# Sharing the copies of a pair of pieces five to three, and pairing pieces across two units in the third block

## The chip, the cores and the metric

The kernel runs on one core of a Trainium2 chip. The metric is the device time of one execution in microseconds (us); several runs are timed and their median is given. One further execution is recorded by the hardware profiler, and all the profile's rows come from it.

## What is computed

An encoder-decoder layer in fp32. The encoder works on 77 context rows per batch; the decoder on 2 batches of 2048 rows of width 512, 16 heads of 32. The change lies in the decoder's causal self-attention:

```python
yn = _ln(y, dec_n1_s, dec_n1_b)
y = y + _mha(yn, yn, dec_sa_in_w, ..., sb)      # sb: relative bias and causal mask
# in _mha:
scores = jnp.einsum('bhqd,bhkd->bhqk', q, k) / jnp.sqrt(hd) + bias[None]
attn = jax.nn.softmax(scores, axis=-1)
out = jnp.einsum('bhqk,bhkd->bhqd', attn, v)
```

After it come cross-attention to the encoder's output and a feed-forward layer, which the change does not touch.

## The kernel before

**Units and pieces.** A batch's 2048 rows are four blocks m = 0 to 3 of 512 rows. The self-attention of a block is cut into 16 *units* (b, m, g, t): g is one of four groups of four heads, t one of four tiles of 128 query rows. Units are numbered through: block 1 of the first batch is units 16 to 31, block 2 ("the third block") 32 to 47, block 3 48 to 63; the second batch's are 64 later. A unit looks at i + 1 = 4m + t + 1 tiles of 128 keys, cut into *pieces* of up to four tiles by `pieces`: in block 2, t = 0 has pieces of 4, 3 and 2 tiles, t = 1 4, 4, 2, t = 2 4, 4, 3 and t = 3 4, 4, 4. Block 3 has four pieces in each unit, block 1 two. `stream` is the list of all pieces in order.

**What is done to a piece.** Four steps, each a function:

- `scores` (L353): one matmul for each of the four heads, each into a PSUM bank of its own. VectorE takes them out (L362, and L369 with the bias for the last two tiles) with a running maximum. After a unit's last piece its four exponentials on ScalarE (L379, one per head over the whole width of the unit) can run; for m > 0 they are put in a list, `late_exps`, and called a few at a time by `exps`.
- `turn` (L389 to L412): transposes the probabilities. A *load* is four transposes (one key tile, four heads) into one bank, and a copy of that bank to `pts`, by ScalarE (L409) or by VectorE (L407). The first half of a turn's loads (rounded up) is ScalarE's. Behind the fourth load's copy one exponential of the next unit is called (L410, L411), and another at the end.
- `values` (L420): the products with `vv`, into the eighth bank, which is kept for them.
- `slot` (called once per unit): other work laid out by hand over the units: projections (L206, L217, L230), the output product (L242), norms, divisions, and in the early units the encoder's stages. Each has its loads by DMA, issued up to three jobs ahead.

**Banks.** `bank()` hands out seven banks in rotation to scores, loads and slots' jobs alike, in the order in which the program calls it. Each engine runs its instructions in the order of the program (`manual_schedule`), and a matmul waits for the engine that last read its bank.

**The main loop** (in the listing below, from L1249) takes up to two pieces of the same unit as a *pair*: it makes sure that the unit is fully scored and its exponentials are called, turns the pair, runs the next unit's slot if the pair ends the unit, scores one more piece ahead if `may_score` allows, calls one exponential (two in block 1), does the pair's values, and after a pair of two scores further pieces as far as `may_score` allows. `may_score` lets a unit be scored where the unit two before it has been turned, as both lie in the same half of `pp`. A unit of block 2 is thus a pair and a left-over piece; a unit of block 3 is two pairs, of which the first is followed by a score directly and the second by a slot.

Of the kernel before, what the change touches and what calls it, by code (L numbers as in the profile page):

```python
# [54 lines left out]
def tile_encoder_decoder(ctx: ExitStack, tc: tile.TileContext, ins, out):  # L55
# [93 lines left out]
    with (  # L149
# [20 lines left out]
        def bank():  # L170

            i = count["bank"] % count["banks"]
            count["bank"] += 1
            return psum[:, i, :]

        def in_turn(what, tile):
            i = count[what] % tile.shape[1]
            count[what] += 1
            return tile[:, i, :]
# [116 lines left out]
        def pieces(i):  # L296


            n = i + 1
            if n % 4 == 1 and n > 1:  # L300
                sizes = [4] * ((n - 5) // 4) + [3, 2]
            else:
                sizes = [4] * (n // 4) + ([n % 4] if n % 4 else [])
            out, k0 = [], 0
            for s in sizes:
                out.append((k0, s))
                k0 += s
            return out

        units = [(b, m, g, t) for b in range(B) for m in range(NMB) for g in range(NC) for t in range(TB)]  # L310
        stream = [(n, k0, kn) for n, u in enumerate(units) for k0, kn in pieces(u[1] * TB + u[3])]
# [17 lines left out]
        late_exps = []  # L329

        def exps(k):

            for _ in range(min(k, len(late_exps))):
                late_exps.pop(0)[1]()
# [54 lines left out]
        def turn(pieces):  # L389

            first = units[pieces[0][0]][1] == 0
            loads = []
            for n, k0, kn in pieces:
                ks = range(k0, k0 + kn)
                if first:
                    loads += [[(n, k, r) for k in ks] for r in range(HC)]
                else:
                    loads += [[(n, k, r) for r in range(HC)] for k in ks]
            for o, load in enumerate(loads):
                pt = bank()  # L400
                pts = in_turn("pts", pts_all).rearrange("p (x q) -> p x q", q=P)
                for x, (n, k, r) in enumerate(load):
                    nc.tensor.transpose(pt[:, ts(x, P)], state[n]["p"][r][:, ts(k, P)], ident)  # L403
                    got[n, k, r] = pts[:, x, :]
                w = len(load) * P
                if o % 2 if first else o >= (len(loads) + 1) // 2:
                    nc.vector.tensor_copy(pts[:, : len(load), :], pt[:, :w])  # L407
                else:
                    nc.scalar.copy(pts[:, : len(load), :], pt[:, :w])  # L409
                if o == min(3, len(loads) - 1):  # L410
                    exps(1)  # L411
            exps(1)  # L412

        def values(n, k0, kn):
            b, m, g, t = units[n]
            i = m * TB + t
            for k in range(k0, k0 + kn):
                ot = psum[:, 7, :].rearrange("p (t q) -> p t q", q=P)
                for r in range(HC):
                    nc.tensor.matmul(  # L420
                        ot[rows4(r), t, :], vv[:, k, ts(g * HC + r, HD)], got.pop((n, k, r)),
                        start=(k == 0), stop=(k == i),
                    )
                if t == TB - 1 and k == i:
                    o = ots[b, m, g] = in_turn("oT", oT_all)
                    (nc.vector.tensor_copy if m else nc.scalar.copy)(o, psum[:, 7, :])
# [459 lines left out]
        ahead = {n: [] for n in range(-1, len(units) + NU)}  # L886

        for x, (b, m) in enumerate(blocks):
            u = x * NU
            first = m == 0  # L890
# [12 lines left out]
            for t in range(TB):  # L903
                end = x == len(blocks) - 1
# [26 lines left out]
        def load_next():  # L931

            while len(loaded) < min(len(queue), ran[0] + (5 if ran[0] < 4 else 3)):
                ahead = [queue[i][2] for i in range(ran[0], len(loaded) + 1)]
                if sum(ahead) > 2:
                    break
                loaded.append(queue[len(loaded)][0]())
# [27 lines left out]
        def slot(n):  # L965
            for f in light[n]:
                f()
            for _, run, _ in jobs[n]:
                load_next()
                run(loaded[ran[0]])  # L970
                ran[0] += 1
# [35 lines left out]
        def w_1_load(i):  # L1007

            nc.sync.dma_start(w_1[:, :, ts(i, D)], wchunk("dec_ff1_wT", i * D))
# [217 lines left out]
        end = len(units)  # L1227
        size = [m * TB + t + 1 for b, m, g, t in units]
        turned_to, scored_to, at = {n: 0 for n in range(end)}, {}, [0]

        def may_score():

            if at[0] == len(stream):
                return False
            n, k0, kn = stream[at[0]]
            same = n >= 2 and units[n][:2] == units[n - 2][:2]
            return n < 2 or turned_to[n - 2] >= (min(k0 + kn, size[n - 2]) if same else size[n - 2])

        def score_next():
            n, k0, kn = stream[at[0]]  # L1240
            scores(n, k0, kn)
            scored_to[n] = k0 + kn
            at[0] += 1
# [4 lines left out]
        i = 0  # L1248
        while i < len(stream):  # L1249
            n = stream[i][0]  # L1250
            pair = [p for p in stream[i : i + 2] if p[0] == n]
            while scored_to.get(n) != size[n]:
                score_next()
            while any(u == n for u, _ in late_exps):
                exps(1)
            ends = pair[-1][1] + pair[-1][2] == size[n]
            if ends:
                for f in ahead[n + 1]:
                    f()
            turn(pair)  # L1260
            if n == end - 2:
                for _, k0, _ in pair:
                    w_1_load(k0 // 4)
            turned_to[n] = pair[-1][1] + pair[-1][2]
            if ends and n + 1 < end:
                slot(n + 1)
            if may_score():
                score_next()
            exps(2 if units[n][1] == 1 else 1)
            for p in pair:  # L1270
                values(*p)
            while may_score() and (len(pair) > 1 or units[n][1] == 0):
                score_next()
            i += len(pair)

# [68 lines left out]
```

## Time and profile before

| what | us |
|---|---|
| median of 3 runs | 2958.81 (2956.04 to 2960.45) |
| the profiled execution: its own time | 2958.76 |
| the profiled execution: span from first to last instruction | 2957.0 |
| block 1, first batch (196.4 to 413.6) | 217.2 |
| block 2, first batch (413.6 to 646.9) | 233.3 |
| block 3, first batch (646.9 to 934.9) | 288.0 |
| blocks 1, 2, 3 of the second batch | 200.5, 233.4, 275.9 |

The cuts are the first transposes of each block; the first batch's blocks hold the encoder's stages and the second's parts of the cross-attention in their slots. The last block is taken to 1785.5, some 5 us after its last transpose; behind it comes the feed-forward phase, to the end. In the profile PE is TensorE's matmul and PEld its weight load, DVE is VectorE, ACT is ScalarE, POOL is GpSimd. A timeline row gives the start, the length, the engine, the line, the operation, output <- input with shapes, how many were merged, and in brackets the engine's idle time ahead of it with what ended it. A row of several merged instructions gives their common length. The granted TensorE clock was 0.987 over the span.

### The profile page before, as it was taken

Reading aid. Unit: us, or ns where it says so; the run is one execution under the profiler, and the core shown is the slowest. Engines: PE = TensorE matmul, PEld = TensorE weight load, DVE = VectorE, ACT = ScalarE, POOL = GpSimd, SP = SyncE. Lnnn points to the kernel's source line nnn. Section 1 sums busy time; section 2 is a strip of 40 time slices with the busy share of each in tenths; the row PEclk is TensorE's granted clock in tenths of the full one; section 3 lists DMA queues with packets and bytes.
Section 4 is the critical chain, followed back from the end, with each engine's and each line's share of the span. In section 5 each row is a group of like instructions: output and inputs, shape, how many; then the busy total and the mean of one; then the engine's idle time right before and its main releaser. Section 6 shows DMA issues by size and latency. Waiting matters only on the chain.

```text
span 2957.0 us, 60689 instructions
## 1 busy us (share of the span) xinstructions
PE 2875.8 (97%) x24440; PEld 2018.7 (68%) x24440; DVE 2202.4 (74%) x6171; ACT 1220.9 (41%) x2211; POOL 737.2 (25%) x601
## 2 busy tenths in 40 slices
PE   8899999999999999999999997999999999999999
PEld 5456666666666556666666675777777777777788
DVE  4767688888987788888878884767676777776765
ACT  3344456546665455555556671213131313131311
POOL 0100000000000101000000004464646464646464
PEclk9799999999999999999999999999999999999999
DMA  6313301201112502201101124000001000000000
GB/s 175 87 52 118 102 16 51 66 16 44 34 41 69 129 19 79 70 26 62 41 16 37 45 75 156 1 29 1 29 1 37 10 29 1 29 1 29 1 15 15
DMA packets 117643, 137.10 MB, mean 46 GB/s; under 512 B 18240, under 2 KB 73072, under 8 KB 117234
## 3 DMA queue, kind: packets, MB, share of 16 engines
q1 hardware_dynamic: 117362, 133.22, 15.5%
q8 instruction: 192, 3.15, 0.5%
q14 instruction: 89, 0.73, 0.1%
HBM read 111.33 MB, written 21.86 MB: 45 GB/s over the span
## 4 chain that ended last, share of the span: by engine, by line
PE 79%; DVE 13%; DMA 3%; issue 2%; POOL 2%; ACT 2%; SPq 0%; POOLq 0%; DVEq 0%; ACTq 0%
PE psum L1152 13%; PE psum L403 12%; PE psum L353 9%; PE psum L1121 8%; PE psum L420 7%; DVE pp L362 5%; PE psum L230 4%; PE psum L806 4%; PE psum L746 4%; PE psum L206 4%; PE psum L242 4%; PE psum L217 3%; DVE pp L369 3%; PE psum L786 2%; PE psum L797 1%
## 5 line engine op out<-in xcount | busy, mean ns | idle before, releaser
L379 ACT ACTIVATE pp<-pp,nm 128x128 f32<-128x128 f32 (+15 forms) x512 | 614.6, 1210 | 200.8 <-DVE nm L376 198.2
L362 DVE TENSOR_SCALAR_CACHE_REDUCE pp<-psum 128x512 f32<-128x512 f32 (+3 forms) x1024 | 558.3, 590 | 47.2 <-PE psum L353 45.3
L403 PE MATMUL psum<-ident,pp 128*128 128x128 f32 x4352 | 549.6, 279 | 18.3 <-DVE mx L369 11.8
L403 PEld LDWEIGHTS psum<-ident,pp 128*128 128x128 f32 x4352 | 475.1, 142 | 132.3 <-DVE pp L362 57.1
L409 ACT COPY pts<-psum 128x512 f32<-128x512 f32 (+3 forms) x592 | 299.1, 577 | 509.6 <-PE psum L403 400.6
L1104 POOL TENSOR_TENSOR vv<-pp 128x512 f32<-128x512 f32 x320 | 415.6, 1316 | 137.4 <-PE psum L1121 117.7
L407 DVE COPY pts<-psum 128x512 f32<-128x512 f32 (+2 forms) x544 | 329.9, 660 | 42.1 <-PE psum L403 39.3
L353 PE MATMUL psum<-kT,q 32*128 32x512 f32 (+3 forms) x2560 | 352.1, 579 | 4.6 <-ACT kT L222 1.6
L420 PEld LDWEIGHTS psum<-pts,vv 128*32 128x32 f32 x8704 | 226.2, 110 | 124.1 <-issue 116.9
L420 PE MATMUL psum<-pts,vv 128*32 128x128 f32 x8704 | 278.7, 275 | 0.2 <-DVE vv L233 0.2
L268 POOL TENSOR_TENSOR rstd<-rstd,mhalf 128x1 f32<-128x1 f32 x32 | 18.2, 570 | 929.8 <-DVE rstd L267 924.4
L1138 DVE TENSOR_TENSOR kT<-kT,psum 128x512 f32<-128x512 f32 x256 | 166.5, 680 | 98.3 <-PE psum L1121 80.5
L1141 ACT ACTIVATE kT<-kT,vecs 128x256 f32<-128x256 f32 x256 | 115.6, 502 | 299.8 <-DVE kT L1138 299.8
L369 DVE CUSTOM_DVE_ANT_0 pp<-psum,bias 128x256 f32<-128x256 f32 (+1 forms) x512 | 209.8, 410 | 20.9 <-PE psum L353 16.6
L353 PEld LDWEIGHTS psum<-kT,q 32*128 32x128 f32 x2560 | 119.4, 184 | 148.6 <-issue 99.4
L1152 PE MATMUL psum<-vv 128*128 128x256 f32 x768 | 176.9, 381 | 0.0
L1121 PE MATMUL psum<-oT,vv 128*128 128x256 f32 x736 | 166.5, 380 | 0.0
L1152 PEld LDWEIGHTS psum<-vv 128*128 128x128 f32 x768 | 143.1, 190 | 26.8 <-issue 9.5
L1121 PEld LDWEIGHTS psum<-oT,vv 128*128 128x128 f32 x736 | 138.8, 190 | 24.4 <-issue 6.2
L1104 DVE TENSOR_TENSOR vv<-kT 128x512 f32<-128x512 f32 x160 | 138.9, 886 | 10.8 <-PE psum L1152 9.9
L253 POOL TENSOR_TENSOR xr<-xr,row_dec_sa_out_b 128x512 f32<-128x512 f32 x32 | 40.7, 1272 | 402.4 <-DMA xr<-in_x_dram 206.3
L1121 PE MATMUL psum<-nT,vv 128*128 128x256 f32 x512 | 119.2, 385 | 16.8 <-POOL vv L1104 15.5
(176 smaller groups left out, 3930.9 us busy)
## 6 DMA issues: line engine op xcount, KB each, us to landing
wqk<-in_dec_sa_in_wT_dram SPq DMA_DIRECT2D x64, 256.0 KB, 3.6
bias<-tz SPq DMA_DIRECT2D x128, 128.0 KB, 3.7
wbig<-in_dec_sa_in_wT_dram SPq DMA_DIRECT2D x8, 1024.0 KB, 7.5
vv<-in_enc_ff_wT_dram SPq DMA_DIRECT2D x8, 1024.0 KB, 5.2
wbig<-in_dec_sa_out_wT_dram SPq DMA_DIRECT2D x8, 1024.0 KB, 7.1
xr<-in_x_dram SPq DMA_DIRECT2D x32, 256.0 KB, 4.5
y<-xr SPq DMA_DIRECT2D x32, 256.0 KB, 2.8
vv<-y SPq DMA_DIRECT2D x32, 256.0 KB, 3.4
```

Of the source, the lines that this page charges most:

```text
L353: nc.tensor.matmul(banks[r][:, : kn * P], q[rows4(r), ts(t, P)], kT[rows4(r), g, k0 * P : (k0 + kn) * P], start=True, stop=True,)
L362: nc.vector.tensor_scalar(p[:, k0 * P : (k0 + far) * P], s[:, : far * P], 1.0, None, ALU.mult, ALU.max, accum_out=st["mx"][:, r, c : c + 1],)
L369: nc.vector.tensor_tensor_reduce(p[:, (i + 1) * P - w : (i + 1) * P], s[:, far * P : kn * P], biases[b, m, g][:, r, 2 * P - w :], 1.0, LOW ...
L379: nc.scalar.activation(p, p, AF.Exp, bias=nm, accum_out=to)
L403: nc.tensor.transpose(pt[:, ts(x, P)], state[n]["p"][r][:, ts(k, P)], ident)
L407: nc.vector.tensor_copy(pts[:, : len(load), :], pt[:, :w])
L409: nc.scalar.copy(pts[:, : len(load), :], pt[:, :w])
L420: nc.tensor.matmul(ot[rows4(r), t, :], vv[:, k, ts(g * HC + r, HD)], got.pop((n, k, r)), start=(k == 0), stop=(k == i),)
L1104: engine.tensor_tensor(dst, quarter(*parts[0], n), quarter(*parts[2], n), SIGN[parts[1]])
L1121: nc.tensor.matmul(mm[:, ts(f, TOK)], a[:, c, ts(f, P)], b[:, c, :], start=(c == 0), stop=(c == 1))
L1138: nc.vector.tensor_tensor(dst, dst, got, SIGN[sign])
L1152: nc.tensor.matmul(mm[:, t, :], lhs[:, c, ts(t, P)], rhs[:, c, :], start=(n == 0 and c == 0), stop=(n == 3 and c == 1),)
```

## The change

First, in `turn`, for blocks 1 to 3: ScalarE copies five loads of a turn of more than four, and two of a smaller one, where it was the first half. Second, in the main loop: in block 2, where a left-over piece belongs to an even t, the next unit's first piece joins it. The next unit then has two pieces left, which make a pair of their own. Per two units there are three turns instead of four. The checks ahead of the turn go over both units of such a pair, and `ends`, which was a flag, now holds the number of the unit whose slot comes next.

```diff
-                if o % 2 if first else o >= (len(loads) + 1) // 2:
+                if o % 2 if first else o >= (5 if len(loads) > 4 else 2):
                     nc.vector.tensor_copy(pts[:, : len(load), :], pt[:, :w])
                 else:
                     nc.scalar.copy(pts[:, : len(load), :], pt[:, :w])
...
             n = stream[i][0]
+            b, m, g, t = units[n]
             pair = [p for p in stream[i : i + 2] if p[0] == n]
-            while scored_to.get(n) != size[n]:
-                score_next()
-            while any(u == n for u, _ in late_exps):
-                exps(1)
-            ends = pair[-1][1] + pair[-1][2] == size[n]
-            if ends:
-                for f in ahead[n + 1]:
-                    f()
+            if m == 2 and len(pair) == 1 and t % 2 == 0:
+
+                pair.append(stream[i + 1])
+            for u in sorted({p[0] for p in pair}):
+                while scored_to.get(u) != size[u]:
+                    score_next()
+                while any(e == u for e, _ in late_exps):
+                    exps(1)
+            ends = n + 1 if any(p[0] == n and p[1] + p[2] == size[n] for p in pair) else None
+            for f in ahead[ends] if ends else ():
+                f()
             turn(pair)
-            if n == end - 2:
-                for _, k0, _ in pair:
+            for u, k0, kn in pair:
+                turned_to[u] = k0 + kn
+                if u == end - 2:
                     w_1_load(k0 // 4)
-            turned_to[n] = pair[-1][1] + pair[-1][2]
-            if ends and n + 1 < end:
-                slot(n + 1)
+            if ends and ends < end:
+                slot(ends)
             if may_score():
                 score_next()
-            exps(2 if units[n][1] == 1 else 1)
+            exps(2 if m == 1 else 1)
             for p in pair:
                 values(*p)
-            while may_score() and (len(pair) > 1 or units[n][1] == 0):
+            while may_score() and (len(pair) > 1 or m == 0):
                 score_next()
             i += len(pair)
```

## The prediction

> Short names: a **load** is four transposes into one PSUM bank and one copy out of it; a **turn** is the loads of one pair of pieces; A.k or D.k is load k's copy on ScalarE or VectorE; **score** is L353's group, **values** L420's. Times after "+" count from a turn's first transpose. Everything is worked against the profiled execution (2958.76 us, its span 2957.0); the median of the runs is 2958.81, so the sum carries over as it is.
>
> **What bounds the kernel now.** First the page's busy shares, then busy time by stage: here blocks 1, 2 and 3 of the first batch, cut at their first transposes.
>
> ```profile
> PE 2875.8 (97%) x24440; PEld 2018.7 (68%) x24440; DVE 2202.4 (74%) x6171; ACT 1220.9 (41%) x2211; POOL 737.2 (25%) x601
> 196.40:413.60 217.20, 213.93 (x1996) 145.16 (x1992) 153.16 (x553) 96.71 (x193) 7.15 (x8) 1.00 0.29 89
> 413.60:646.90 233.30, 232.16 (x2554) 152.34 (x2553) 196.94 (x654) 136.79 (x215) 7.14 (x8) 1.00 0.14 42
> 646.90:934.90 288.00, 284.40 (x3420) 195.52 (x3416) 246.26 (x796) 177.28 (x257) 7.14 (x8) 0.99 0.13 39
> ```
>
> The columns of the last three are PE, PEld, DVE, ACT, POOL, then clock, DMA share and GB/s. PE is busy 98 to 99.5% of each block at full clock; DVE has 84 to 86% in blocks 2 and 3, ACT 59 to 62%. So a PE wait is lost in full, and only PE waits can be won. How a turn runs is read from the timeline. The first turn of unit 52 (block 3, t = 0):
>
> ```profile
> 728.81 3.54 PEld L403 LDWEIGHTS psum<-ident,pp 128*128 128x128 f32 x32 [0.33 <-issue]
> 729.50 2.05 ACT L409 COPY pts<-psum 128x512 f32<-128x512 f32 x4 [6.97 <-DVE oT L426]
> 731.42 1.82 ACT L379 ACTIVATE pp<-pp,nm 128x1792 f32<-128x1792 f32 x1
> 731.54 2.48 DVE L407 COPY pts<-psum 128x512 f32<-128x512 f32 x4
> 732.51 0.31 PEld L353 LDWEIGHTS psum<-kT,q 32*128 32x128 f32 x8 [0.17 <-issue]
> 733.21 1.80 ACT L379 ACTIVATE pp<-pp,nm 128x1792 f32<-128x1792 f32 x1
> 733.59 1.69 PEld L420 LDWEIGHTS psum<-pts,vv 128*32 128x32 f32 x64 [0.76 <-issue]
> ```
>
> Eight loads take 3.70, the score 1.08, then come the values. ACT makes A.0 to A.3 (+0.69 to +2.74), and then an exponential of 1.82, put behind the fourth copy by L410. D.4 to D.7 run meanwhile. What a score does when it needs banks that ACT still reads is seen at unit 40:
>
> ```profile
> 532.99 2.02 ACT L409 COPY pts<-psum 128x512 f32<-128x512 f32 x4
> 533.63 0.29 PEld L353 LDWEIGHTS psum<-kT,q 32*128 32x128 f32 x2 [0.17 <-ACT pts L409]
> 534.09 0.29 PEld L353 LDWEIGHTS psum<-kT,q 32*128 32x128 f32 x2 [0.17 <-ACT pts L409]
> 534.58 0.29 PEld L353 LDWEIGHTS psum<-kT,q 32*128 32x128 f32 x2 [0.19 <-ACT pts L409]
> 535.07 0.29 PEld L353 LDWEIGHTS psum<-kT,q 32*128 32x128 f32 x2 [0.20 <-ACT pts L409]
> 536.12 0.48 PEld L420 LDWEIGHTS psum<-pts,vv 128*32 128x32 f32 x20 [0.76 <-DVE pts L407]
> ```
>
> Each of the four matmuls (a weight pair each) waits for one copy; the last starts 0.06 after the last copy (535.01), and the values 1.05 after that. The score took 2.49 instead of 1.08: such a wait passes to PE undiminished.
>
> **Moved copies.** By the loops, VectorE's copies fall from 96 to 48 in block 1, 160 to 96 in block 2, 224 to 144 in block 3 (both batches): 192 in all, 0.60 each on DVE (2.48 for four, less overlap), 115 us; on ACT they take 0.48 each, 92 us. The Trainium skill, Perfetto Trace Analysis, section Identifying the Most-Contended Engine, says not to judge TensorE by matmul busy time but by weight-load busy and MFU. By weight loads PE stands at 65 to 68% in these blocks, DVE at 84 to 86% is the most contended, and taking 115 us off it could bring up to that, 2844. The rows speak otherwise: transposes follow at 0.11 each (3.54 for 32), with nothing between groups but the 0.2 to 0.8 "issue" gaps, which no copy ends. I go by the rows.
>
> Does DVE's relief help PE? DVE is late only in a burst of score evictions just ahead of a turn: 3.71, 4.40, 4.57 and 3.64 pass until the score in units 52 to 55, where 3.64 is the undisturbed turn. But that burst starts after a slot (jobs of 3.6 us on PE) in which DVE runs dry: in unit 25 it idles 5.18 ahead of L245, in unit 51 2.39 ahead of L208. A copy saved before that gap shortens the gap. I put the gain in block 1 and in second turns of block 3 at 0 (ends: -6, +2). Nothing is lost there: 3.6 us of jobs lie between the turn and the next score, and cover a copy that is 2.3 late.
>
> **The fifth copy in turns of eight loads without a slot.** Seven banks go round: loads take j to j+6 and j again, the score j+1 to j+4. Its fourth matmul needs load 4's bank, freed by D.4 so far (+3.42 in unit 52, before the score at +3.70). Now A.4 frees it, and A.4 stands behind the exponential. Exponentials start at +2.61; A.4 starts 0.03 before their end, lasts 0.58, PE follows 0.06 later: 3.22 + d. With d = 1.82, 1.93, 2.04, 1.71 for t = 0 to 3 (units 52 to 55): 5.04, 5.15, 5.26, 4.93, against 3.71, 4.40, 4.57, 3.64. Loss 1.33 + 0.75 + 0.69 + 1.29 = 4.06 per four units. The old DVE waits are contained in it: they end sooner than A.4. Block 3 has 8 such fours; the last two units of each batch have no score there (-4.0): **+28.5**. Behind the waiting matmul stand the values and the next turn on PE; behind A.4 the next exponentials, 0.5 later, which end at about +8.5, while the next turn's first copy moves to about +9.8. Ends: 20 (part of the burst moves too) and 36 (burst on top).
>
> **The merged turns of block 2.** (a) *t = 0.* The next unit's first piece is turned straight after the values of the first turn, so its four exponentials must be done. Unit 36's row of exponentials is 1.36 apart. New ACT queue: A.0-A.3, exp 0 (+2.61 to +3.99), A.4 (to +4.44), exps 1 to 3, end +8.52; PE may go at +8.58. PE is there at 477.04 - 471.10 = +5.94, plus 8 + 3 transposes of 0.109: +7.14. Before, the slot's 3.6 us and a score lay between. Wait 1.44, eight times: **+11.5**. (b) *Unit 47 and its twin* (no score between): exps 1.58 apart end at +9.4; PE comes at 5.91 + 15 x 0.109 = +7.5: 2 x 2.0 = **+4.0**. Other t = 2 merges have a score more and longer cover (arrival +10.3 against +9.5): 0. (c) *t = 2, first turn*: the fifth copy, 3.22 + 1.61 = 4.83, against scores at 4.00 (units 34, 42 and twins; 38 is at 5.35 already): 4 x 0.83 = **+3.3**. (d) *t = 1*: two scores follow each other and then six loads at once, without the slot that let DVE evict. At 0.61 to 0.72 per eviction I get 1.5 lost where the double score loses 1.1 now: 8 x 0.4 = **+3** (ends -4, +12). (e) Unit 40's wait of 1.41 came from an exponential ahead of A.0; that order is gone: 2 x **-1.4**. (f) Sixteen fewer turns: 32 + 8 transposes and 64 + 16 values now take 3.64 + 0.82 + 1.88 + 0.57, two groups of 24 and 48 take 2 x (2.67 + 1.45), and so on: 0.23 per four units, **-1.8**. A turn itself costs nearly nothing. No score has to be forced: by the loop the next unit is always scored by then. No DMA is added; slots keep their order and run up to 1.7 us later, under loads issued three jobs ahead. Sum of block 2: **+17.2**.
>
> **Sum.** 2958.8 + 28.5 + 17.2 + 0 = 3004.5; I say 3004.
>
> **Rivals.**
> - *Merging is free* (15%): ACT is ahead, or (a), (b), (d) are covered by DVE's relief. Only the fifth copy and its like count: 2958.8 + 28.5 + 3.3 - 4.6 = 2986. For it: ACT is idle 40% of block 2. Against: the exponentials can't start before their maxima, which come at the end of the turn before.
> - *Everything adds* (11%): the burst waits return on top of A.4 (8 x 1.7 = 14): 3018. Against: DVE has less to do.
> - *Faster* (5%): PE waits for DVE, and relief reaches the burst. Its place is the transposes of the first turns: 8 x 1.76 in block 3, 8 x 1.6 in block 1 (3.37 for 2.67, 3.95 for 3.06 in units 25 and 26), 2 x 2.8 in block 2: 32 us, 2926. It decides if A.4 is done by the score, at +3.7: only with exponentials under 0.5 us, which are 1.7 to 2.0.
> - *It does nothing* (4%): the score's banks are waited for as one anyway. Unit 40's paced pairs and D.4 ending before each score speak against.
>
> **Numbers.** Likeliest 3004 (65%, own range 2993 to 3014). The range 2982 to 3021 takes in the free merge and most of the heavy case. A measurement here tells 0.2% (6 us) from no change: faster 0.05, same 0.04, slower 0.91.
>
> **What would show it.** Right: scores in block 3 whose last weight pair starts 0.06 after the fifth ACT copy ends, 0.7 to 1.3 late, waiting for L409; block 3 longer by some 14 us per batch, block 2 by 9, block 1 unchanged; transposes of t = 1 units waiting for L379 by 1.4; DVE busy less by 115, ACT more by 92. Wrong: block 1 shorter by several us (relief does reach PE), or A.4 ahead of the exponential, which would take most of the loss away.

## The result, and the profile after

| | us |
|---|---|
| before, median of 5 | 2958.6 |
| after, median of 5 (3011.54 to 3014.45) | 3011.8 |
| ratio, 95% interval | 1.0186 [1.0172, 1.0200] |
| predicted | 3004, range 2982 to 3021 |

The change makes the kernel slower by 53 us, where 45.7 was forecast. Busy shares of the changed kernel, and its blocks 1, 2 and 3 of the first batch, cut as before (PE, PEld, DVE, ACT, POOL, clock, DMA, GB/s):

```profile
PE 2910.8 (97%) x24440; PEld 2030.0 (67%) x24440; DVE 2107.9 (70%) x5979; ACT 1311.2 (44%) x2403; POOL 735.6 (24%) x601
198.80:416.00 217.20, 213.93 (x1996) 145.19 (x1992) 141.08 (x529) 108.24 (x217) 7.15 (x8) 1.00 0.29 89
416.00:666.90 250.90, 242.99 (x2577) 157.53 (x2576) 185.38 (x641) 152.81 (x248) 7.15 (x8) 0.99 0.13 39
666.90:960.40 293.50, 289.39 (x3393) 194.50 (x3392) 220.99 (x737) 195.51 (x295) 7.14 (x8) 1.00 0.13 37
```

VectorE is relieved by 94.5 us and ScalarE takes on 90, and nothing is won. Block 1 takes 217.2 as before, with 12 us less on VectorE. By the unrounded cuts block 2 is 17.6 longer and block 3 5.4 (second batch: 17.9 and 9.2). The first turn of unit 52 in the changed kernel, the one shown in the prediction:

```profile
743.62 3.54 PEld L403 LDWEIGHTS psum<-ident,pp 128*128 128x128 f32 x32 [0.33 <-issue]
744.36 2.05 ACT L409 COPY pts<-psum 128x512 f32<-128x512 f32 x4 [6.54 <-DVE oT L426]
746.27 1.82 ACT L379 ACTIVATE pp<-pp,nm 128x1792 f32<-128x1792 f32 x1
746.50 1.89 DVE L407 COPY pts<-psum 128x512 f32<-128x512 f32 x3
747.33 0.30 PEld L353 LDWEIGHTS psum<-kT,q 32*128 32x128 f32 x6 [0.17 <-issue]
747.33 1.13 PE L353 MATMUL psum<-kT,q 32*128 32x512 f32 x6
748.06 0.60 ACT L409 COPY pts<-psum 128x512 f32<-128x512 f32 x1
748.71 0.29 PEld L353 LDWEIGHTS psum<-kT,q 32*128 32x128 f32 x2 [1.08 <-ACT pts L409]
748.72 1.12 PE L353 MATMUL psum<-kT,q 32*128 32x512 f32 x2 [0.25 <-ACT pts L409]
749.76 0.27 PEld L420 LDWEIGHTS psum<-pts,vv 128*32 128x32 f32 x12 [0.76 <-issue]
```

The transposes take 3.71 as before. Of the score's eight weight loads six go at 747.33; the last pair stands until the fifth copy, which follows the exponential, ends at 748.66. The score takes 2.43 instead of 1.08. VectorE's three copies are done by 748.39, earlier than the bank for which PE waits.

The two PE rows show what the wait does. Before, the four heads' matmuls of this score ran side by side:

```profile
732.52 1.14 PE L353 MATMUL psum<-kT,q 32*128 32x512 f32 x8
```

Now three heads run side by side in 1.13, PE is idle for 0.25, and the fourth head's matmul runs alone for 1.12. So most of what is lost is counted as busy. This is why the page's PE busy time rises by 35 though PE does the same 24440 matmuls: it rises by 33 to 36 in the three kernels in which scores wait for the fifth copy (this one, e1 and e7 below) and by at most 4.3 in the others. Such a loss must be looked for in the timeline. The other cost, at the merged turn of units 36 and 37:

```profile
481.98 1.38 ACT L379 ACTIVATE pp<-pp,nm 128x1280 f32<-128x1280 f32 x1
482.18 1.07 PEld L403 LDWEIGHTS psum<-ident,pp 128*128 128x128 f32 x10 [0.20 <-issue]
483.32 1.37 ACT L379 ACTIVATE pp<-pp,nm 128x1280 f32<-128x1280 f32 x1
483.50 0.14 PEld L403 LDWEIGHTS psum<-ident,pp 128*128 128x128 f32 x1 [0.24 <-ACT pp L379]
484.83 1.40 PEld L403 LDWEIGHTS psum<-ident,pp 128*128 128x128 f32 x13 [1.20 <-ACT pp L379]
```

Eight transposes are unit 36's, then unit 37's begin; its third head waits 0.24 and its fourth 1.20 for that head's exponential. The wait sums to 1.44.

### The profile page after: what moved, and what is told of

Read it like the earlier page. It is cut to its first block, busy times and chain, and to the rows that moved or that the text cites. A ratio compares the mean times of both kernels' runs of the same rounds, so it can differ in the third digit from the quotient of the medians.

```text
span 3010.0 us, 60829 instructions
## 1 busy us (share of the span) xinstructions
PE 2910.8 (97%) x24440; PEld 2030.0 (67%) x24440; DVE 2107.9 (70%) x5979; ACT 1311.2 (44%) x2403; POOL 735.6 (24%) x601
## 4 chain that ended last, share of the span: by engine, by line
PE 78%; DVE 12%; ACT 4%; issue 2%; DMA 2%; POOL 2%; SPq 0%; ACTq 0%; POOLq 0%; DVEq 0%
PE psum L1152 13%; PE psum L403 12%; PE psum L353 9%; PE psum L1121 8%; PE psum L420 7%; DVE pp L362 4%; PE psum L806 4%; PE psum L230 4%; PE psum L206 4%; PE psum L746 4%; PE psum L242 4%; PE psum L217 3%; DVE pp L369 3%; ACT pp L379 2%; PE psum L786 2%
## 5 line engine op out<-in xcount | busy, mean ns | idle before, releaser
L379 ACT ACTIVATE pp<-pp,nm 128x128 f32<-128x128 f32 (+15 forms) x512 | 619.0, 1218 | 155.4 <-DVE nm L376 152.8
L409 ACT COPY pts<-psum 128x512 f32<-128x512 f32 (+3 forms) x784 | 407.1, 586 | 526.1 <-PE psum L403 402.2
L362 DVE TENSOR_SCALAR_CACHE_REDUCE pp<-psum 128x512 f32<-128x512 f32 (+3 forms) x1024 | 559.1, 590 | 97.4 <-PE psum L353 93.0
L403 PE MATMUL psum<-ident,pp 128*128 128x128 f32 x4352 | 556.1, 280 | 29.7 <-DVE mx L369 13.4
L353 PE MATMUL psum<-kT,q 32*128 32x512 f32 (+3 forms) x2560 | 375.8, 577 | 6.5 <-ACT pts L409 2.9
L407 DVE COPY pts<-psum 128x512 f32<-128x512 f32 (+3 forms) x352 | 214.8, 649 | 82.7 <-PE psum L403 80.8
L353 PEld LDWEIGHTS psum<-kT,q 32*128 32x128 f32 x2560 | 126.8, 183 | 167.3 <-issue 94.3
L369 DVE CUSTOM_DVE_ANT_0 pp<-psum,bias 128x256 f32<-128x256 f32 (+1 forms) x512 | 209.6, 409 | 21.6 <-PE psum L353 20.8
```

The lines of the kernel that those rows point to most:

```text
L353: nc.tensor.matmul(banks[r][:, : kn * P], q[rows4(r), ts(t, P)], kT[rows4(r), g, k0 * P : (k0 + kn) * P], start=True, stop=True,)
L362: nc.vector.tensor_scalar(p[:, k0 * P : (k0 + far) * P], s[:, : far * P], 1.0, None, ALU.mult, ALU.max, accum_out=st["mx"][:, r, c : c + 1],)
L369: nc.vector.tensor_tensor_reduce(p[:, (i + 1) * P - w : (i + 1) * P], s[:, far * P : kn * P], biases[b, m, g][:, r, 2 * P - w :], 1.0, LOW ...
L379: nc.scalar.activation(p, p, AF.Exp, bias=nm, accum_out=to)
```

## Experiments

Theory: the change costs through two waits of PE, for a bank that the fifth copy holds behind an exponential, and for exponentials that the merged turns need too early; VectorE's relief is worth nothing. Rivals: only one of the two parts costs; the number of ScalarE's copies costs, whichever they are; the relief is worth something and is hidden by the waits.

| run | median | before on that chip | ratio, 95% interval | expected |
|---|---|---|---|---|
| copies alone (e1) | 3001.75 | 2959.3 | 1.0147 [1.0130, 1.0164] | 2999 |
| merged turns alone (e2) | 2973.04 | 2959.3 | 1.0050 [1.0035, 1.0065] | 2971 |
| all, fifth copy is the last load (e3) | 2981.65 | 2959.3 | 1.0077 [1.0062, 1.0092] | 2976 |
| all, exponential behind the fifth copy (e4) | 2976.79 | 2959.3 | 1.0061 [1.0046, 1.0076] | 2976 |
| copies alone, exponential behind (e5) | 2956.4 | 2958.9 | 0.9997 [0.9988, 1.0005] | 2958 |
| all, slot ahead of merged turns (e7) | 3001.39 | 2958.9 | 1.0148 [1.0133, 1.0163] | 2996 |
| all, both mendings (e8) | 2964.78 | 2958.9 | 1.0023 [1.0014, 1.0033] | 2961 |
| both mendings, one score (e9) | 2963.05 | 2958.9 | 1.0016 [1.0008, 1.0023] | 2955 to 2961 |

Beside the medians a second measure is used: the time from a unit's first transpose to the next unit's, in the trace, against the kernel before. In blocks 1 to 3, units that an edit does not touch agree between two traces to 0.01 us; in block 0 of the first batch single units differ by up to 3.

**Each part alone.** The kernel before, with one of the two hunks:

```diff
-                if o % 2 if first else o >= (len(loads) + 1) // 2:
+                if o % 2 if first else o >= (5 if len(loads) > 4 else 2):
```

> The five-to-three copies alone, no merged turns. Theory (the fifth copy stands behind an exponential and holds a bank that the next score needs): block 3 loses per four units what it lost in the changed kernel, 4.05, some 30 us in both batches; block 2 loses in its t = 2 and t = 3 first turns, about 10; block 1 nothing. About 2999. Rival 1 (the merged turns are what costs): about 2962, block 3 unchanged. Rival 2 (VectorE's relief is worth something where nothing waits): block 1 shorter by several us.

3001.75. Block 3's units 52 to 55 lose 1.37, 0.74, 0.67 and 1.28, together 4.06 (4.05 in the changed kernel); block 2 is longer by 5.1 and 5.0, in its t = 2 units by 0.82 (units 38 and 46 by nothing) and in t = 3 by 1.34 to 1.38 (unit 47 by nothing). Block 1 changes by -0.05 and -0.55. The first rival is out.

The other hunk alone is the changed kernel with the copies shared as before:

```diff
-                if o % 2 if first else o >= (5 if len(loads) > 4 else 2):
+                if o % 2 if first else o >= (len(loads) + 1) // 2:
```

> The merged turns alone, copies shared half and half. Theory: t = 0 merges wait for exponentials by 1.44 less the 0.48 of the fifth copy, 0.96 each (8), unit 47 and its twin 1.5 each (3), the run of scores in t = 1 about 0.75 more per four units (6), unit 40's old wait gone (-2.8), fewer groups (-1.8): about 2971, block 3 unchanged but for the scores that move from its first unit to the end of block 2. Rival (merging is free, the fifth copy is all): 2959 or less, no wait of transposes for exponentials.

2973.04, so merging isn't free: units 36 and 37 together lose 2.2, 34 and 35 0.3. From unit 49 on block 3 is as before to 0.01, but its first unit is 6.8 shorter and block 2's last one 13.4 longer: scores of block 3 are now taken at the end of block 2. The two costs, 42.5 and 13.7, add to 56, 3 more than both parts in one kernel. The units of blocks 2 and 3 show 1.6 of this (40.0 and 11.7 against 50.1), as the balance of two things: the t = 3 turns, where the copies alone lose 1.35 in six places, are followed by a slot once turns are merged and lose nothing more, while the t = 0 merges and the end of block 2 lose more with the added copies than without.

**Is it the bank, or ScalarE's queue?** Two ways to free the score's bank in time, with the number of copies on each engine as in the change. Both are edits of the changed kernel; the first is e3, the second e4:

```diff
-                if o % 2 if first else o >= (5 if len(loads) > 4 else 2):
+                if o % 2 if first else (4 <= o < len(loads) - 1 if len(loads) > 4 else o >= 2):
```

```diff
-                if o == min(3, len(loads) - 1):
+                if o == min(4 if len(loads) > 4 else 3, len(loads) - 1):
```

> The whole change, but ScalarE's fifth load is the turn's last one instead of its fifth in order: as many copies on each engine, the same exponential between the fourth and fifth of them, but a bank that the next score does not need. Theory (bank held): the score's waits vanish, block 3 is as before; left are block 2's waits for exponentials (11.5 + 4) and run of scores (6) less 4.6: about 2976. Rival (ScalarE's longer queue or VectorE's order costs, whichever bank it is): stays near 3011.

> The whole change, but the exponential is called behind the fifth copy instead of ahead of it. Theory (what matters is when the fifth bank is free): the fifth copy ends at +3.2, ahead of the score, block 3 is as before, about 2976; the exponentials' chain in block 2 is no shorter, so the waits of the t = 0 merges stay at 1.4. Rival (the copies cost by their number on ScalarE): stays near 3011. If relief of VectorE is worth something, this one shows it: block 3 shorter than before.

Block 3's units 49 to 59 stand within 0.15 of the kernel before in both. In the second, units 36 and 37 still lose 2.3: the wait for exponentials is a cost of its own. In the first (e3), ScalarE runs four copies, the exponential and the fifth copy just as in the change, but that copy empties the last load's bank. Unit 52's first turn there:

```profile
738.87 2.05 ACT L409 COPY pts<-psum 128x512 f32<-128x512 f32 x4 [6.54 <-DVE oT L426]
740.78 1.82 ACT L379 ACTIVATE pp<-pp,nm 128x1792 f32<-128x1792 f32 x1
741.89 0.31 PEld L353 LDWEIGHTS psum<-kT,q 32*128 32x128 f32 x8 [0.17 <-issue]
742.57 0.61 ACT L409 COPY pts<-psum 128x512 f32<-128x512 f32 x1
742.97 0.59 PEld L420 LDWEIGHTS psum<-pts,vv 128*32 128x32 f32 x24 [0.76 <-issue]
```

All eight weight loads go at 741.89, ahead of the fifth copy, and the score takes 1.08. It is the bank. The median of e3 is 5.6 above its expectation; its profiled execution was the fastest of the four (2977.18). The units of blocks 2 and 3 show 18.9 more than before, 2.4 of it in unit 126, where a late last copy meets the values directly; the rest of the median lies outside them and is not explained.

**Is VectorE's relief worth anything?** On the kernel before, the first edit of this section (the five-to-three copies) and e4's (the exponential behind the fifth copy).

> No merged turns; ScalarE takes five copies, and the exponential is called behind the fifth. Theory (the copies cost only through the bank, and VectorE's relief is worth nothing since it falls into its idle stretch in the slot): as before within 2 us, about 2958, although VectorE does some 190 copies less. Rival (relief helps, the exponential's place hid it): 2930 to 2950, with fewer waits of transposes for L362 and L369 in blocks 1 and 3.

2956.4, ratio 0.9997 [0.9988, 1.0005]: no difference. Blocks 1 and 3 of the first batch:

```profile
198.50:415.70 217.20, 213.92 (x1996) 145.13 (x1992) 141.07 (x529) 107.98 (x217) 7.15 (x8) 1.00 0.29 89
648.70:936.50 287.80, 284.29 (x3420) 195.90 (x3416) 226.74 (x756) 196.49 (x297) 7.14 (x8) 0.99 0.13 39
```

VectorE is busy 12.1 and 19.5 less than before in them, and they take 217.2 and 287.8 against 217.2 and 288.0. Nor do PE's waits in block 3 go: weight loads of transposes wait 17.0 for L362 and 6.4 for L369, where it was 17.4 and 7.4 before. The time saved falls into VectorE's idle stretches, as the row of unit 51's slot shows, before and in this run:

```profile
707.35 0.75 DVE L208 TENSOR_SCALAR q<-psum,vecs 128x512 f32<-128x512 f32 x1 [2.39 <-PE psum L206]
709.58 0.75 DVE L208 TENSOR_SCALAR q<-psum,vecs 128x512 f32<-128x512 f32 x1 [2.64 <-PE psum L206]
```

Without merged turns VectorE does 176 copies less, not 190, and is 91.6 us less busy in the whole run.

**Do the merged turns wait for want of cover?**

On the changed kernel:

```diff
+            early = pair[0][0] != pair[-1][0]
+            if early:
+                slot(ends)
             turn(pair)
...
-            if ends and ends < end:
+            if ends and ends < end and not early:
                 slot(ends)
```

> The whole change, but in a merged turn the next unit's slot is run ahead of the turn instead of behind it. Theory (a merged t = 0 turn waits for the next unit's exponentials, because the slot no longer covers them): the eight waits of 1.44 and the two of 2.0 are covered by 3.6 us of jobs, 15 us less: about 2996. Rival (the merge costs by its run of scores on VectorE, not by the exponentials): 3008 to 3012.

3001.39: 10.4 less than the change, not 15. Units 36 and 37 lose 0.87 together in place of 2.27, which is the 1.4 expected; the eight t = 0 merges give back 1.2 to 1.7 each, 11.2 in all. Unit 36's exponentials and the merged turn:

```profile
482.55 1.37 ACT L379 ACTIVATE pp<-pp,nm 128x1280 f32<-128x1280 f32 x1
...
484.92 0.14 PEld L403 LDWEIGHTS psum<-ident,pp 128*128 128x128 f32 x1 [0.24 <-issue]
485.35 2.54 PEld L403 LDWEIGHTS psum<-ident,pp 128*128 128x128 f32 x23 [0.29 <-issue]
```

The last exponential ends at 483.92, under the slot's matmuls, and no transpose waits for L379. Unit 47 and its twin, with the units next to them, give back 2.4 instead of 4.0. The last two units of the second batch lose 2.8 more than in the change; why was not found. Together that is 10.8.

**Both mendings, and the run of scores.** e8 is the slot ahead of merged turns and the exponential behind the fifth copy; e9 also scores only one more piece after a merged turn:

```diff
-            while may_score() and (len(pair) > 1 or m == 0):
+            more = 1 if early else len(stream)
+            while may_score() and more and (len(pair) > 1 or m == 0):
                 score_next()
+                more -= 1
```

> The whole change with both mendings: the slot ahead of a merged turn, and the exponential behind the fifth copy. Theory: both costs are gone and the run of scores in t = 1 is left: 2961, no faster than before, since fewer turns save only 2 us. Rival (fewer turns and VectorE's relief are a gain once the waits are gone): 2940 or less.

> As the kernel with both mendings, but after a merged turn only one more piece is scored instead of all that may be. Theory: the run of two scores before the t = 1 turn, 0.7 us each in eight places, is gone unless it comes back one turn later: 2955 to 2961. Rival (the runs of scores are harmless): the same as the kernel with both mendings.

2964.78 and 2963.05. With both waits gone 47 of the 53 us are back, and no version beats the kernel before: three turns for four, arranged like this, save nothing. Of e8's 6 us the units of blocks 2 and 3 show 2.1, mainly in units 32 to 35, their twins and the end of the second batch's block 2; the rest lies outside these blocks, where single executions differ by as much, and is left open. e9 takes 0.74 off units 36 and 37 and gives 0.55 back in 38 and 39: the run of two scores does cost, and returns one turn later. That is too little to tell by the medians.

## Why the prediction was right

| step | forecast | measured, by units of the trace |
|---|---|---|
| block 1 (both) | 0 | -0.05, -0.54 |
| fifth copy, units 52 to 55 | 1.33, 0.75, 0.69, 1.29 | 1.36, 0.74, 0.67, 1.28 |
| block 3 without its first unit (both) | 28.5 - 2 x 1.33 = 25.8 | 29.7 |
| wait for exponentials, t = 0 | 1.44 | 1.44 |
| fifth copy at t = 2 (units 34, 42, twins) | 0.83 | 0.25 |
| unit 47's wait | 2.0 | 1.4 |
| block 2 with block 3's first unit (both) | 17.2 + 2 x 1.33 = 19.9 | 20.4 |
| all of it | 45.7 | 53.2 by medians |

- **What bounds the kernel.** Right. The copies alone with the exponential behind (e5) are the direct test: 91.6 us off VectorE won nothing, so VectorE, at 84 to 86%, did not bound blocks 2 and 3, although PE's weight loads stood at only 65 to 68%. The estimate by weight-load busy time (up to 2844) would have had the sign wrong; MFU, the other measure named in the prediction, was not worked out. Two details were off. VectorE's relief was put at 115: the copies' own rows shrink by 115, but its busy time by 94.5, since its rows overlap in the profile. And a saved copy does not shorten VectorE's idle gap ahead of L208, it lengthens it (2.39 to 2.64).
- **The fifth copy.** Right to 0.03 in each of the four kinds of units, for its size, its place and its reason; two runs that free the bank in two ways take it away. Not read was that PE is idle for only 0.25 of it: the rest is the fourth head's matmul running alone.
- **Second turns of block 3, forecast at 0.** Wrong for the last units of the second batch, whose slots are empty: unit 123's second turn is followed by a score directly, so that the unit loses 2.55 instead of 1.29; unit 126 has no score, and loses 2.7 because the values of its second turn wait for the fifth copy, which stands behind an exponential:

```profile
1820.16 2.07 ACT L379 ACTIVATE pp<-pp,nm 128x2048 f32<-128x2048 f32 x1
1822.16 0.64 ACT L409 COPY pts<-psum 128x512 f32<-128x512 f32 x1
1822.85 0.59 PEld L420 LDWEIGHTS psum<-pts,vv 128*32 128x32 f32 x24 [2.31 <-ACT pts L409]
```

These two make 4.0 of the 3.9 by which block 3 exceeds its forecast; smaller differences nearly cancel.
- **The merged turns.** The wait at t = 0 is right. Unit 47's is smaller than forecast:

```profile
637.59 0.97 PEld L403 LDWEIGHTS psum<-ident,pp 128*128 128x128 f32 x9 [1.41 <-ACT pp L379]
```

The exponentials end 9.4 after unit 46's first transpose, as forecast, but PE gets there at 8.1 instead of 7.5, because that turn's transposes had already waited 0.57 longer for VectorE. The same 0.57 stands in unit 34's first turn, with the copies shared as before too; the fifth copy adds only 0.25 there, where 0.83 were forecast. The run of scores at t = 1, put at 0.4 more than before, is 0.7 to 0.9 (2.27 less 1.44 in units 36 and 37; e9 takes 0.74 away). Units 40 and 41 lose 1.7 less than 36 and 37, their twins 1.4 less, where unit 40's old wait was put at 1.4. That the sum of block 2 comes so close (20.4 for 19.9) is in part luck: the fifth copy at t = 2 and unit 47's wait are together 3.5 below their forecasts, the runs of scores some 3.5 above.
- **The blocks' shares.** "Block 3 longer by some 14 per batch, block 2 by 9" is wrong: 5.4 and 9.2, and 17.6 and 17.9 were measured. Up to three scores in a row, which belonged to unit 48, are now taken behind unit 47, so that unit 47 is 15.0 longer and unit 48 7.9 shorter. The sum does not suffer: with unit 48 counted to block 2 the two parts are 20.4 and 29.7.
- **The rest.** The start, block 0 and the phase after the attention hold the remaining 3 us; the change leaves the work there alone, and single executions differ there by as much.

"Merging is free" is refuted by its own run; "everything adds" by units 53 and 54, where the burst's wait and the copy's overlap (0.74 and 0.67 lost, not some 1.5 each); "faster" by the run in which the exponential no longer hides the relief; "it does nothing" by the result.

## What to carry to other kernels

Before work is moved from a busy engine to an idle one, look at what the moved instruction will stand behind on the new engine's queue, and who waits for the buffer that it frees: here an engine idle 40% of the time held a PSUM bank 1.3 us too long, because an exponential came first. When matmuls run side by side, one that comes late costs nearly its whole length again: 1.12 here, in which the engine counts as busy. Relief of an engine counts only if its backlog reaches the bottleneck; VectorE ran dry between its bursts, so saved work only lengthened its idle stretch. And where a queue's order is written by hand, the place of an instruction can be worth more than its engine: one line that puts the exponential behind the copy took the whole cost of the shared copies away.

## What was not expected

PE's busy time grew by 35 us with the same instructions, so that its share stayed at 97% in both kernels, while the kernel lost 53 us. Units of blocks 1 to 3 that an edit leaves alone repeat to 0.01 us from trace to trace, but executions of the kernel before range from 2952.7 to 2961.9; in the traces such differences lie in block 0 of the first batch and behind the last unit (up to 5.2 us between two kernels with the same program there), not in those units.
